# Expert layer of a two-layer decoder: where the first half's norms stand, two tiles opened in the attention before, a table of zeros filled later

## The chip, the cores and the metric

The kernel runs on one core of one Trainium2 chip. The metric is device time in microseconds of one launch. A core has five engines that work beside one another, each on its own queue in order: TensorE (PE, matrix products, with its weight loads shown apart as PEld), VectorE (DVE), ScalarE (ACT), GpSimd (POOL) and SyncE (SP, which here only issues transfers). An instruction waits at the head of its queue until the semaphores that it needs have been raised, and all behind it wait too. Data come and go by DMA engines.

## The reference, cut to what matters

The whole is a decoder of two layers on 16 sequences of 128 tokens, width 512: a state-space layer, a cross attention, a ternary feed-forward, a self attention, a gated attention over a memory, and a layer of experts. In the layer norm, `_layernorm`, mean and variance of a token are taken over the 512 values. The change touches the cross attention's start, the gated attention's end and the experts.

The experts come in 8 groups of 8. A router picks 8 experts for each token and gives each a weight. A token takes part in a group if one of its experts is in it: the token plus a mask projection (`mask_up_w`, chosen by which experts of the group were picked) goes through the group's gated product, `silu(g) * u` with inner width 352, and is brought back to 512. The results of its groups are weighed and added to the token, and the sum is normalised and written out.

## The kernel before

**Stages.** `stage_ssm`, `stage_xattn`, `stage_ffn`, `stage_attention` (self attention, then gated attention) and `stage_moe` follow one another. A sequence of 128 tokens is one tile of 128 partitions. The 16 sequences stay on the chip as `x`. Single precision products run in two passes, so that a product of 128x512 shows as two records.

**Who sets the order.** The kernel is written in generators. Each advances by one `yield` for each tick of the stage's loop, so that the jobs are mixed by hand. What is written is then ordered on each engine by a list scheduler, which may move an instruction a good deal ahead or back of its place in the text, with one exception: instructions passed to `tc.keep_in_program_order` stay among one another, and with what is around them, where they were written. Pools of buffers (`tile_pool`, `bufs=`) decide when a buffer comes free.

**Zeros.** `clear_rows` (L396) is a job that `stage_xattn` starts first (L642). It makes a table of zeros in memory, in eight transfers on SP's queue, and from the table fills the expert buckets: `bucket[half][group]`, 768 rows of 776 values, in six transfers each, and one row of each `results[half][group]`. In the same loop `project` (L479) loads the context `cT` of a sequence on SP's queue (L481), and makes `pk` and `pv` from it (L491). The keys are normalised and rotated on VectorE, ScalarE and GpSimd; the tables of cosine and sine come from `sincos` (L351 to L369).

**Experts.** The first half's tokens (sequences 0 to 7) are routed while the gated attention runs. `route` computes the weights, and GpSimd scatters each token's row to its group's bucket. Those of sequences 8 to 15 are routed in `stage_moe`. A row has 512 values, 256 picks, and 8 weights. The unit of work in `stage_moe` is a tile of 128 rows. There are 98 units: six for each of the 8 groups of both halves, but for the last group of the second half, which is done directly on the 8 sequences. Each unit goes through the steps below, and at tick t of the loop each step works on another unit, at a fixed lag:

```python
for lag, what in ((-5, m.fetch), (-1, m.turn_in), (0, m.gate_up), (1, m.turn_act), (-2, m.masks), (-3, m.places), (2, m.down), (2, m.store)):
```

`fetch` loads the row tile (`row`, six buffers, on SP). `places` turns the picks (`pts` on TensorE, `soft` on ScalarE). `masks` is the product `pm` on TensorE and the addition `xg` on VectorE. `turn_in` transposes (`ptx`, then `xgT` on ScalarE). `gate_up` makes `pg` and `pu` with sixteen passes, `Silu` on ScalarE and `act` on VectorE. `turn_act` transposes `act`. `down` makes `y`. `store` copies it to `yo` on VectorE and writes it to `results`.

When a group is done, `combine` (L1572) gathers the results per token on GpSimd (`got`) and, three parts later, adds them to `x` (L1584). For the last group and an odd sequence it goes on to `finish`: `layernorm` of two sequences on VectorE (20 instructions: two statistics each, the reciprocal root of `rsqrt`, two scalings) and two output transfers on SP. The scheduler is free to place these VectorE instructions. In the first half there are four such pairs.

The Moe object holds `k.to_route` (the sequences to be routed), `tick` and `send` (the parts of that job), and the weights of the first group (`m.first`), which are loaded in `stage_attention`. The pool of `stage_moe` is opened at its start, when those of the attention have been closed, and takes their memory; its row loads wait for that. Between the attention and the experts the row load of the first tile is issued on SP at 2459.91 us of the span.

Of the kernel before, what the change touches and what calls it, by code (L numbers as in the profile page):

```python
# [10 lines left out]
F32 = mybir.dt.float32  # L11
BF16 = mybir.dt.bfloat16
F32R = mybir.dt.float32r
I32 = mybir.dt.int32
U8 = mybir.dt.uint8
AF = mybir.ActivationFunctionType
ALU = mybir.AluOpType
# [3 lines left out]
P = 128  # L21
NB = 16
D = 512
# [19 lines left out]
        self.n += 1  # L43


def rsqrt(k, v, n, eps, scale=1.0):


    nc = k.nc
    a = k.small.tile([P, n], F32, tag=f"rs_a{n}", name="rs_a")  # L50
    y = k.small.tile([P, n], F32, tag=f"rs_y{n}", name="rs_y")
    t = k.small.tile([P, n], F32, tag=f"rs_t{n}", name="rs_t")
    nc.vector.tensor_scalar(a, v, scale, eps, ALU.mult, ALU.add)
    nc.vector.tensor_scalar(y.bitcast(I32), a.bitcast(I32), -0.5, 1597463007.0, ALU.mult, ALU.add)
    for _ in range(3):
        nc.vector.tensor_tensor(t, y, y, ALU.mult)
        nc.vector.scalar_tensor_tensor(t, t, -0.5, a, ALU.mult, ALU.mult)
        nc.vector.scalar_tensor_tensor(y, t, 1.5, y, ALU.add, ALU.mult)
    return y


def layernorm(k, ins, outs, eps=1e-5):

    nc, n = k.nc, len(ins)
    mv = k.small.tile([P, n, 2], F32, tag=f"ln_mv{n}", name="ln_mv")
    for i, r in enumerate(ins):
        st = k.small.tile([P, nc.vector.BN_STATS_DIM], F32, tag="ln_st", name="ln_st")
        nc.vector.bn_stats(st, r)
        nc.vector.bn_aggr(mv[:, i, :], st)
    rstd = rsqrt(k, mv[:, :, 1], n, eps)  # L70
    for i, (r, o) in enumerate(zip(ins, outs)):
        nc.vector.tensor_scalar(o, r, mv[:, i, 0:1], rstd[:, i : i + 1], ALU.subtract, ALU.mult)


def stage_ssm(k):
# [320 lines left out]
def clear_rows(k, pool):  # L396

    n = Moe.ROW // 8
    zero = pool.tile([P, n], F32, name="zero")
    k.nc.gpsimd.memset(zero, 0.0)  # L400
    for i in range(8):
        k.nc.sync.dma_start(k.zeros[:, i * n : (i + 1) * n], zero)
    yield
    for h in range(2):
        for bucket, result in zip(k.bucket[h], k.results[h]):
            k.nc.sync.dma_start(result[0:1], k.zeros[0:1, 0:D])
            for j in range(Moe.TILES):
                k.nc.sync.dma_start(bucket[j * P : (j + 1) * P], k.zeros)
                yield
# [830 lines left out]
def stage_attention(k):  # L1240

    nc, tc = k.nc, k.tc
    U = 8
    with ExitStack() as ctx:
        wk = ctx.enter_context(tc.tile_pool(name="s4w", bufs=2))
        own = ctx.enter_context(ExitStack())
        wr = own.enter_context(tc.tile_pool(name="s4r", bufs=2, side="right"))  # L1250
        pp = ctx.enter_context(tc.tile_pool(name="s4p", bufs=2, space=PSUM))
        psc = ctx.enter_context(tc.tile_pool(name="s4s", bufs=1, space=PSUM))
        ppt = ctx.enter_context(tc.tile_pool(name="s4t", bufs=1, space=PSUM))
        pao = ctx.enter_context(tc.tile_pool(name="s4o", bufs=1, space=PSUM))
        pools = wk, wr, pp, psc, ppt, pao
        pairs = [c(k, p, pools) for c in (SelfAttention, GatedAttention) for p in range(NB // 2)]
        units = [(pr, n) for pr in pairs for n in range(U)]

        begin = {}
        for m, pr in enumerate(pairs):  # L1260
            begin.setdefault(U * m - (14 if m < NB // 2 else 10), []).append(pr)
        running = [load_gated_weights(k)]
        first = [pairs[0].project(), pairs[1].project()]
        for n in range(12):
            next(first[0])
            if n >= 7:
                next(first[1])
        running.append(first[1])
        for t in range(-2, len(units) + 2):
            if k.moe:  # L1270
                k.moe.tick()
            for lag in (2, 1, 0, -1, -2):
                if not 0 <= t - lag < len(units):
                    continue
                pr, n = units[t - lag]
                if lag == pr.LAG:
                    pr.turn(n)
                    if n % 4 == 3:
                        running.append(pr.values(n // 4))
                if lag == 1:  # L1280
                    pr.norm(n)
                if lag == 0:
                    pr.exps(n)
                if lag == -1 and n % 2 == 0:
                    pr.top(n)
                if lag == -2 and n % 2 == 0:
                    pr.scores(n)
            if t == NB // 2 * U + 20:
                own.close()
                k.moe = Moe(k, pp)  # L1290
                running.append(k.moe.setup())
            for pr in begin.get(t, []):
                if t > -2:
                    running.append(pr.project())
            for job in list(running):
                if next(job, running) is running:
                    running.remove(job)
            if k.moe:
                k.moe.tick()
                k.moe.send()  # L1300
        while running:
            k.moe.tick()
            for job in list(running):
                if next(job, running) is running:
                    running.remove(job)
            k.moe.tick()
            k.moe.send()


class Moe:  # L1310
# [199 lines left out]


    def fetch(self, u):
        u.row = self.wk.tile([P, self.ROW], F32, tag="row", name="row", bufs=6)
        self.nc.sync.dma_start(u.row, u.src)

    def places(self, u):
        at = D + P * (u.g // 4)
# [3 lines left out]
        self.nc.scalar.copy(u.soft, pt)  # L1521

    def masks(self, u):
        pm = self.pm.tile([P, D], F32, tag="pm", name="pm")
        self.nc.tensor.matmul(pm, u.soft, self.mup[u.g], start=True, stop=True)
        u.xg = self.wk.tile([P, D], F32, tag="xg", name="xg")
        self.nc.vector.tensor_tensor(u.xg, pm, u.row[:, 0:D], ALU.add)
# [43 lines left out]
    def combine(self, h, g, n):  # L1571

        k, nc, b = self.k, self.nc, h * (NB // 2) + n
        got = self.wk.tile([P, D], F32, tag="got", name="got", bufs=10)

        end = 1 + min(P * (n + 1), self.CAP)
        nc.gpsimd.indirect_dma_start(  # L1577
            out=got[:, :], out_offset=None, in_=k.results[h][g][0:end, :],
            in_offset=bass.IndirectOffsetOnAxis(ap=self.gidx[:, b, g : g + 1], axis=0),
        )  # L1580
        yield
        yield
        yield
        nc.gpsimd.tensor_tensor(k.x[b], got, k.x[b], ALU.add)  # L1584
        for _ in range(4):
            yield
        if g == self.NG - 1 and n % 2:
            self.finish(b - 1)

    def finish(self, b):  # L1590
        xs = self.k.x[b : b + 2]
        layernorm(self.k, xs, xs)
        for i, x in enumerate(xs):
            self.nc.sync.dma_start(self.k.args["out"][b + i], x)


def stage_moe(k):


    nc, tc, m = k.nc, k.tc, k.moe  # L1600
    NG, T, H = m.NG, m.TILES, NB // 2
    with ExitStack() as ctx:
        m.wk = wk = ctx.enter_context(tc.tile_pool(name="s6w", bufs=2))
        wp = ctx.enter_context(tc.tile_pool(name="s6m", bufs=2))
        mp = ctx.enter_context(tc.tile_pool(name="s6u", bufs=1))
        m.pgu = ctx.enter_context(tc.tile_pool(name="s6g", bufs=1, space=PSUM))
# [3 lines left out]
        units, weights = [], {0: m.first}  # L1610
        for h in range(2):
            for g in range(NG):
                last = h and g == NG - 1
                for j in range(H if last else T):
                    u = Ctx()
                    u.h, u.g, u.j, u.b = h, g, j, H + j
                    u.src, u.to = (k.rows[u.b][:, :], None) if last else (
                        k.bucket[h][g][j * P : (j + 1) * P, :], k.results[h][g][1 + j * P : 1 + (j + 1) * P, :]
                    )
                    units.append(u)  # L1620
        running = []
# [3 lines left out]
                if next(job, running) is running:  # L1625
                    running.remove(job)

        for t in range(-5, len(units) + 4):
            if t == 3:
                k.to_route += range(H // 2, H)  # L1630
            m.tick()
            n = t + 8
# [4 lines left out]
            for lag, what in ((-5, m.fetch), (-1, m.turn_in), (0, m.gate_up), (1, m.turn_act), (-2, m.masks), (-3, m.places), (2, m.down), (2, m.store)):  # L1637
                if not 0 <= t - lag < len(units):
                    continue
                u = units[t - lag]  # L1640
                if what == m.fetch:
                    u.w = None
                if what == m.gate_up:
                    u.w = weights[u.h * NG + u.g]
                what(u)
            if 0 <= t - 3 < len(units) and units[t - 3].to is not None:
                u = units[t - 3]
# [17 lines left out]
        with tc.If(over > 0):  # L1665
            for b in range(NB):
                nc.sync.dma_start(k.x[b], k.rows[b][:, 0:D])
            for g in range(NG):
                w = m.load(wp, g)
                for b in range(NB):  # L1670
                    u = Ctx()
# [131 lines left out]
```

## Time and profile before

| what | value |
|---|---|
| three runs | 3347.26, 3347.7, 3352.11 us, median 3347.7 |
| profiled execution | 3354.11 us |
| its span | 3352.3 us (1.8 us lie around it) |
| mean granted TensorE clock | 0.969 |
| busy: PE, DVE, ACT, POOL | 94%, 56%, 41%, 41% of the span |
| cross attention begins | about 607 us |
| experts begin | about 2463 us |

A row of a timeline has start, duration, engine, line, operation, output and inputs, shape, and in square brackets the idle time ahead of it and the instruction or transfer that released it. A row of the waits has the sum, the number and the longest. A row of the windows has for each engine its busy time in a stretch; the clock is 1.00 at full speed, and the two last columns are DMA share and GB/s. The times of PE's ends are modelled, so neighbouring products overlap a little.

### The profile page before, as it was taken

How to read it: one execution, taken by the hardware profiler on the slowest of the kernel's cores; microseconds unless marked ns; L12 is line 12 of the kernel's file. 1: busy time of each engine (PE TensorE's matmuls, PEld its weight loads, DVE VectorE, ACT ScalarE, POOL GpSimd, SP SyncE). 2: the span in 40 equal slices, each digit the busy share in tenths (PEclk: the TensorE clock that was granted, in tenths of full speed). 3: DMA queues.
4: the chain of work that ended last, by engine and by line, in shares of the span. 5: the costliest groups of instructions: out<-in, count | busy, mean ns of one | idle time of the engine just before them, and what ended most of it. 6: DMA issues, size and time to landing. Idle time of an engine off the chain costs nothing.

```text
span 3352.3 us, 38574 instructions
## 1 busy us (share of the span) xinstructions
PE 3160.3 (94%) x12944; PEld 1814.2 (54%) x12944; DVE 1874.6 (56%) x4202; ACT 1381.0 (41%) x3299; POOL 1390.2 (41%) x1196
## 2 busy tenths in 40 slices
PE   6899998899999999999999899998989999999998
PEld 3444444355555555555566466665555566556665
DVE  5887788556456456455576589665643332322224
ACT  4655555233333333334433399765632322112221
POOL 6977886233333233232000265225624454233331
PEclk8999999899999999999999999998999999999999
DMA  6533332780000000002200100023345575445441
GB/s 231 135 80 96 85 87 63 242 293 4 7 4 7 4 4 7 4 1 101 85 1 1 63 1 1 14 71 135 136 144 181 190 242 198 156 157 171 162 157 64
DMA packets 162577, 317.28 MB, mean 95 GB/s; under 512 B 20233, under 2 KB 83209, under 8 KB 159300
## 3 DMA queue, kind: packets, MB, share of 16 engines
q1 hardware_dynamic: 124164, 216.23, 20.9%
q0 software_dynamic: 19200, 64.16, 5.6%
q10 hardware_dynamic: 19008, 34.35, 2.7%
q8 instruction: 105, 1.72, 0.2%
q14 instruction: 100, 0.82, 0.1%
HBM read 238.80 MB, written 129.04 MB: 110 GB/s over the span
## 4 chain that ended last, share of the span: by engine, by line
PE 64%; DVE 9%; ACT 3%; DMA 2%; issue 2%; POOL 2%; SPq 0%; ACTq 0%; POOLq 0%; DVEq 0%
PE pq L491 6%; PE y L1558 6%; PE pg L1541 6%; PE pu L1541 6%; PE po L614 6%; PE po L781 4%; PE pk L491 3%; PE ao L603 3%; PE sc L563 3%; PE pt L377 3%; PE pv L491 2%; PE ps L1142 2%; PE pg L767 2%; PE pu L767 2%; PE pT L591 1%
## 5 line engine op out<-in xcount | busy, mean ns | idle before, releaser
L245 POOL TENSOR_TENSOR dBx<-dtx,BC 128x1024 f32<-128x1024 f32 x128 | 301.9, 2378 | 33.2 <-DVE h L258 26.0
L1541 PE MATMUL pg<-gu,xgT 128*128 128x352 f32 x784 | 301.2, 466 | 0.0
L1541 PE MATMUL pu<-gu,xgT 128*128 128x352 f32 x784 | 300.4, 465 | 0.0
L1558 PE MATMUL y<-dn,aT 128*128 128x512 f32 x588 | 268.3, 592 | 0.0
L1545 DVE SCALAR_TENSOR_TENSOR act<-pu,row,act 128x352 f32<-128x352 f32 x98 | 57.1, 583 | 377.2 <-PE pu L1541 319.0
L583 POOL TENSOR_TENSOR pr<-pr,sm 128x512 f32<-128x512 f32 x128 | 134.7, 1053 | 289.5 <-DVE sm L582 235.0
L236 ACT ACTIVATE h<-dt,negA 128x254 f32<-128x254 f32 x512 | 239.9, 474 | 15.0 <-DVE dt L178 2.1
L1584 POOL TENSOR_TENSOR x<-got,x 128x512 f32<-128x512 f32 x120 | 152.3, 1275 | 224.5 <-DMA got<-results,gidx 220.4
L614 PE MATMUL po<-w,aT 128*128 128x512 f32 x512 | 230.6, 593 | 0.5 <-DVE aT L608 0.5
L491 PE MATMUL pq<-w,xT 128*128 128x512 f32 x512 | 228.9, 594 | 0.0
L1577 POOL DMA_INDIRECT got<-results,gidx x120 | 116.2, 968 | 270.1 <-DMA results<-yo 193.9
L468 POOL TENSOR_TENSOR m<-m,m 128x512 f32<-128x512 f32 x96 | 121.6, 1267 | 244.0 <-DVE m L463 244.0
L576 ACT ACTIVATE pr<-sc,mx,sf 128x256 f32<-128x256 f32 x256 | 142.9, 562 | 188.1 <-DVE mx L569 175.8
L258 DVE TENSOR_TENSOR_SCAN h<-h,dBx 128x1024 f32<-128x1024 f32 x80 | 183.3, 2294 | 57.7 <-ACT h L236 43.1
L267 PE MATMUL py<-hC,ident 128*128 128x512 f32 x320 | 167.9, 654 | 41.6 <-ACT y L272 35.5
L1541 PEld LDWEIGHTS pu<-gu,xgT 128*128 128x128 f32 x784 | 151.1, 193 | 84.9 <-issue 3.8
L1541 PEld LDWEIGHTS pg<-gu,xgT 128*128 128x128 f32 x784 | 144.1, 194 | 65.1 <-issue 3.7
L1544 ACT ACTIVATE act<-pg 128x352 f32<-128x352 f32 x98 | 45.5, 464 | 317.9 <-PE pg L1541 249.6
L1558 PEld LDWEIGHTS y<-dn,aT 128*128 128x128 f32 x588 | 104.1, 190 | 100.8 <-issue 94.0
L1533 ACT COPY xgT<-ptx 128x512 f32<-128x512 f32 x98 | 57.5, 587 | 232.9 <-PE ptx L377 206.1
L491 PEld LDWEIGHTS pq<-w,xT 128*128 128x128 f32 x512 | 93.5, 190 | 102.0 <-issue 99.0
L614 PEld LDWEIGHTS po<-w,aT 128*128 128x128 f32 x512 | 94.7, 190 | 95.3 <-issue 91.8
(363 smaller groups left out, 6824.0 us busy)
## 6 DMA issues: line engine op xcount, KB each, us to landing
bucket<-zeros SPq DMA_DIRECT2D x96, 388.0 KB
row<-bucket SPq DMA_DIRECT2D x90, 388.0 KB
BC<-bcd SPq DMA_DIRECT2D x128, 256.0 KB
results<-yo ACTq DMA_DIRECT2D x90, 256.0 KB
gu<-in_moe_guT SPq DMA_DIRECT2D x16, 1408.0 KB
cT<-in_ctxT SPq DMA_DIRECT2D x32, 256.0 KB
dn<-in_moe_downT SPq DMA_DIRECT2D x16, 512.0 KB
rows<-r_row SPq DMA_DIRECT2D x16, 388.0 KB
```

Source lines behind the costliest of these rows:

```text
L236: nc.scalar.activation(h[:, c, :, 1:], st.dt[:, c].rearrange("p (b t) -> p b t", b=BQ)[:, :, 1:], AF.Exp, scale=negA[:, c, n : n + 1])
L245: nc.gpsimd.tensor_tensor(dBx, st.dtx, BC[:, 0].unsqueeze(1).to_broadcast([P, KC, TQ]), ALU.mult)
L258: nc.vector.tensor_tensor_scan(hf, hf, df, 0.0, ALU.mult, ALU.add)
L267: nc.tensor.matmul(st.py[c], k.ident, st.hC[n][:, 2 * c : 2 * c + 2], start=n == 0, stop=n == NS - 1)
L491: nc.tensor.matmul(ps, src[:, c], w[c], start=c == 0, stop=c == KC - 1)
L576: nc.scalar.activation(pr[:, j], st.sc[g, i][:, j], AF.Exp, scale=st.sf[:, h : h + 1], bias=st.mx[g, i][:, j : j + 1], accum_out=sm[:, j : ...
L583: nc.gpsimd.tensor_tensor(pr, pr, sm.unsqueeze(2).to_broadcast([P, 2, 2 * P]), ALU.mult)
L614: nc.tensor.matmul(st.po, aT[:, j], k.wo[h // 8][:, h % 8], start=h == 0, stop=h == G * J - 1)
L767: nc.tensor.matmul(p, sn.qT[i][:, c], w[:, c, h * D : (h + 1) * D], start=c == 0, stop=c == KC - 1)
L1541: nc.tensor.matmul(ps, u.xT[:, c], gu[:, c, lo : lo + I], start=c == 0, stop=c == KC - 1)
L1558: self.nc.tensor.matmul(u.y, u.aT[:, c], u.w[1][:, c], start=c == 0, stop=c == 2)
L1584: nc.gpsimd.tensor_tensor(k.x[b], got, k.x[b], ALU.add)
```

## The change

There are three parts. `finish` for the first half is written two parts later, and with the rest of the norm is held to its written place by `keep_in_program_order`. `Moe.open`, a new job, is started in `stage_attention` eight units before the end of its loop: it opens a pool of its own with room for two rows, fetches the first two tiles and does `places`, `masks` and `turn_in` for both, with the attention's accumulators; `stage_moe` leaves out these steps for them and starts its loop at −3 instead of −5. And `clear_rows` yields three times before it fills the table of zeros. The arithmetic is the same. On TensorE some 90 places at the border of attention and experts change their order; on VectorE the norms' instructions stand later; on SP the first `cT` load stands ahead of the eight transfers of zeros.

```diff
 def clear_rows(k, pool):
     n = Moe.ROW // 8
+    for _ in range(3):
+        yield
     zero = pool.tile([P, n], F32, name="zero")
...
+            if t == len(units) - 8:
+                assert not (k.moe.now or k.moe.sending or k.to_route)
+                running.append(k.moe.open())
         while running:
...
     def fetch(self, u):
-        u.row = self.wk.tile([P, self.ROW], F32, tag="row", name="row", bufs=6)
+        u.row = self.wk.tile([P, self.ROW], F32, tag="row", name="row", bufs=self.depth)
         self.nc.sync.dma_start(u.row, u.src)
+
+    def open(self):
+
+        self.wk = self.k.moe_ctx.enter_context(self.k.tc.tile_pool(name="s6o", bufs=2, side="right"))
+        self.pm, self.depth, self.opened = self.pp, 2, []
+        for j in range(2):
+            u = Ctx()
+            u.g, u.src = 0, self.k.bucket[0][0][j * P : (j + 1) * P, :]
+            self.opened.append(u)
+            self.fetch(u)
+        yield
+        yield
+        for link in (self.places, self.masks, self.turn_in):
+            for u in self.opened:
+                link(u)
+                yield
...
         if g == self.NG - 1 and n % 2:
-            self.finish(b - 1)
-
-    def finish(self, b):
+            for _ in range(2):
+                yield
+            self.finish(b - 1, k.tc.keep_in_program_order)
+
+    def finish(self, b, keep=lambda ins: ins):
         xs = self.k.x[b : b + 2]
-        layernorm(self.k, xs, xs)
+        layernorm(self.k, xs, xs, keep=keep)
...
-        m.wk = wk = ctx.enter_context(tc.tile_pool(name="s6w", bufs=2))
+        m.wk, m.depth = ctx.enter_context(tc.tile_pool(name="s6w", bufs=2)), 6
...
-                    u = Ctx()
+                    u = Ctx() if len(units) >= len(m.opened) else m.opened[len(units)]
...
-        for t in range(-5, len(units) + 4):
+        for t in range(-3, len(units) + 4):
...
                 u = units[t - lag]
+                if u in m.opened and what in (m.fetch, m.places, m.masks, m.turn_in):
+                    continue
```

In `layernorm` and `rsqrt` each VectorE instruction is passed through `keep`; their default leaves it as it is.

More of the change, by code (lines that the diff above doesn't have):

```diff
@@ L43, in __call__, with rsqrt @@
         self.n += 1
-def rsqrt(k, v, n, eps, scale=1.0):
+def rsqrt(k, v, n, eps, scale=1.0, keep=lambda ins: ins):
     nc = k.nc
@@ L52, in rsqrt, with layernorm @@
     t = k.small.tile([P, n], F32, tag=f"rs_t{n}", name="rs_t")
-    nc.vector.tensor_scalar(a, v, scale, eps, ALU.mult, ALU.add)
-    nc.vector.tensor_scalar(y.bitcast(I32), a.bitcast(I32), -0.5, 1597463007.0, ALU.mult, ALU.add)
+    keep(nc.vector.tensor_scalar(a, v, scale, eps, ALU.mult, ALU.add))
+    keep(nc.vector.tensor_scalar(y.bitcast(I32), a.bitcast(I32), -0.5, 1597463007.0, ALU.mult, ALU.add))
     for _ in range(3):
-        nc.vector.tensor_tensor(t, y, y, ALU.mult)
-        nc.vector.scalar_tensor_tensor(t, t, -0.5, a, ALU.mult, ALU.mult)
-        nc.vector.scalar_tensor_tensor(y, t, 1.5, y, ALU.add, ALU.mult)
+        keep(nc.vector.tensor_tensor(t, y, y, ALU.mult))
+        keep(nc.vector.scalar_tensor_tensor(t, t, -0.5, a, ALU.mult, ALU.mult))
+        keep(nc.vector.scalar_tensor_tensor(y, t, 1.5, y, ALU.add, ALU.mult))
     return y
-def layernorm(k, ins, outs, eps=1e-5):
+def layernorm(k, ins, outs, eps=1e-5, keep=lambda ins: ins):
     nc, n = k.nc, len(ins)
@@ L67, in layernorm @@
         st = k.small.tile([P, nc.vector.BN_STATS_DIM], F32, tag="ln_st", name="ln_st")
-        nc.vector.bn_stats(st, r)
-        nc.vector.bn_aggr(mv[:, i, :], st)
-    rstd = rsqrt(k, mv[:, :, 1], n, eps)
+        keep(nc.vector.bn_stats(st, r))
+        keep(nc.vector.bn_aggr(mv[:, i, :], st))
+    rstd = rsqrt(k, mv[:, :, 1], n, eps, keep=keep)
     for i, (r, o) in enumerate(zip(ins, outs)):
-        nc.vector.tensor_scalar(o, r, mv[:, i, 0:1], rstd[:, i : i + 1], ALU.subtract, ALU.mult)
+        keep(nc.vector.tensor_scalar(o, r, mv[:, i, 0:1], rstd[:, i : i + 1], ALU.subtract, ALU.mult))
 def stage_ssm(k):
@@ L1523, in masks @@
     def masks(self, u):
-        pm = self.pm.tile([P, D], F32, tag="pm", name="pm")
+        pm = self.pm.tile([P, D], F32, tag="pp" if self.pm is self.pp else "pm", name="pm")
         self.nc.tensor.matmul(pm, u.soft, self.mup[u.g], start=True, stop=True)
```

## The prediction, made before the changed kernel had run

> **What bounds the kernel now.** I read the page first (span, slices, chain), then TensorE's waits, then the timeline round the three longest waits that the change touches, and last the granted clock there. Line numbers are those of the kernel before.
>
> ```profile
> span 3352.3 us, 38574 instructions
> PE   6899998899999999999999899998989999999998
> PEclk8999999899999999999999999998999999999999
> PE 64%; DVE 9%; ACT 3%; DMA 2%; issue 2%; POOL 2%; SPq 0%; ACTq 0%; POOLq 0%; DVEq 0%
> ```
>
> TensorE is busy in nearly every slice and carries most of the chain. So an edit pays only where TensorE stands still, or runs at a lower clock after having stood still. Its waits, in all and at the longest:
>
> ```profile
> PE ptx L377 <- DVE xg L1527: 18.7, 9, 6.8
> PE pk L491 <- DMA results<-zeros: 13.2, 1, 13.2
> PE pts L1519 <- DMA row<-bucket: 5.1, 1, 5.1
> PE ptx L377 <- ACT r_x L1410: 4.4, 1, 4.4
> ```
>
> The first three are the norms, the zeros and the start of the experts: one for each part of the change. The norms, on the timeline (start, duration, idle before and its releaser):
>
> ```profile
> 2904.88 1.27 POOL L1584 TENSOR_TENSOR x<-got,x 128x512 f32<-128x512 f32 x1 [6.00 <-DMA got<-results,gidx]
> 2906.18 0.69 DVE L68 BATCH_NORM_STATS2 ln_st<-x 128x6 f32<-128x512 f32 x1 [7.78 <-POOL x L1584]
> 2909.91 0.63 PE L377 MATMUL ptx<-ident,xg 128*128 128x128 f32 x4 [2.75 <-DVE xg L1527]
> ...
> 2936.20 3.73 POOL L1584 TENSOR_TENSOR x<-got,x 128x512 f32<-128x512 f32 x3 [1.27 <-DMA got<-results,gidx]
> 2937.50 0.69 DVE L68 BATCH_NORM_STATS2 ln_st<-x 128x6 f32<-128x512 f32 x1 [6.26 <-POOL x L1584]
> 2946.81 1.09 PE L377 MATMUL ptx<-ident,xg 128*128 128x128 f32 x4 [6.81 <-DVE xg L1527]
> ```
>
> Read it as a chain: VectorE has a norm at the head of its queue and waits for GpSimd's last addition. Behind the norm stand act and xg of the running tiles, and TensorE waits for xg. Five ptx waits lie here (0.72, 2.75, 0.72, 1.83, 6.81 us). The clock pays again:
>
> ```profile
> 2911.00:2914.40 3.40, 3.40 (x7) 1.92 (x6) 0.00 (x0) 0.22 (x1) 0.59 (x1) 0.51 0.33 122
> 2945.20:2952.00 6.80, 5.19 (x12) 3.48 (x13) 2.06 (x4) 0.59 (x1) 1.26 (x1) 0.50 0.73 249
> ```
>
> The column before the last two is the clock: half speed for 3.4 us after the gap of 2.75, for 6.8 us after that of 6.81.
>
> **Part C, the norms (17.5 us).** From the ptx at 2889.25 to the one at 2957.82 are 68.57 us for six tiles; an undisturbed tile takes 8.42 us (2957.82 to 2966.24). 68.57 − 6 × 8.42 = 18.05 us lost: 12.83 in the five waits, the rest by the clock. After the change the norms keep their written place, and in the changed program's order each pair's norm stands about ten tiles later, near 2990 and on. The last addition ended at 2939.93, so nothing is waited for. The same instructions run, 20 on VectorE a pair; in an earlier block they take 0.69 + 0.18 for one tile and then 4.12 us from the second BATCH_NORM_STATS2 to the end, about 4.9 us. They go into this hole of VectorE:
>
> ```profile
> 2958.02 0.69 DVE L1568 COPY yo<-y 128x512 f32<-128x512 f32 x1 [1.99 <-PE y L1558]
> 2963.25 0.58 DVE L1545 SCALAR_TENSOR_TENSOR act<-pu,row,act 128x352 f32<-128x352 f32 x1 [4.54 <-PE pu L1541]
> ```
>
> A hole of 4.54 us takes a block of 4.9 with some 0.4 left over. Act and xg are that much later; xg ends at 2964.44, and TensorE needs it for the load at 2965.81, 1.4 us of slack. Two of the four blocks may cost 0.4 us if they are interleaved worse. The eight output transfers move on SP to a place ahead of a later row load, which is due five tiles ahead: nothing. Gain 18 − 0.5 = 17.5, range 14 to 18.
>
> **Part B, two tiles opened early (8 us).**
>
> ```profile
> 2458.62 1.26 POOL L1230 TENSOR_TENSOR x<-x,gate 128x512 f32<-128x512 f32 x1 [5.65 <-DVE gate L1229]
> 2459.91 1.27 SPq L1514 DMA_DIRECT2D row<-bucket  x3
> 2462.96 0.45 PE L1519 MATMUL pts<-ident,row 128*128 128x128 f32 x1 [5.15 <-DMA row<-bucket]
> ```
>
> The row loads wait for the attention's buffers, and so for its last GpSimd operation; TensorE is idle from 2457.81. Then it goes 0.40 and 0.48 us idle between pts, pm and ptx, with the clock at half from about 2460.5 to 2470.7. In the changed order the rows of tiles 0 and 1 are fetched while the gated attention runs. That attention's loads have come by then, and the scatter that fills the bucket is issued for the last time at 2412.62, some 23 us before TensorE reaches the new pts (behind the transposes at 2435.34). Ahead of the attention's end TensorE gets 2 pts (0.22), 2 pm (0.62), 2 ptx of four transposes each (0.86) and half of tile 0's gate and up (2.37), 4.07 us. Of that about 3.7 falls into its small waits there (0.87, 1.42, 0.73, 0.70 us), so the attention ends about 0.35 later. The other half of gate and up (2.37) runs in the idle 5.15. Tile 1 then waits for VectorE's act of tile 0, which is ordered inside the attention's last norm, until about 2463.7, and for the row of tile 2, which is still issued behind the last GpSimd operation.
> What before has reached at 2476.15 is reached some 11 us earlier if only work counts. Two takings off: a shorter clock loss remains (a gap of about 2 us), and the row of tile 3 queues behind gu and dn (1408 and 704 KB on SP), which land near 2470: 3 us. Net 8, from 4 (only the 5.15 us less a new wait) to 11.
>
> **Part A, the zeros (0.5 us).**
>
> ```profile
> 610.04 8.15 SPq L402 DMA_DIRECT2D zeros<-zero  x8
> 618.24 0.43 SPq L481 DMA_DIRECT2D cT<-in_ctxT  x1
> 621.33 6.75 PE L491 MATMUL pk<-w,cT 128*128 128x512 f32 x8 [13.17 <-DMA results<-zeros]
> ...
> 639.43 0.66 PE L377 MATMUL pt<-ident,m 128*128 128x128 f32 x4 [0.34 <-POOL m L526]
> ```
>
> Eight issues on SP, 8.15 us, and the small packets behind them stand ahead of cT, the real releaser of pk. Put ahead of them, cT comes only behind the second weight load, which fills the queues until about 614.3: pk starts at about 617.2, 4.1 earlier. But the next wait is already there: the second pt (639.43) needs GpSimd's m, at the end of a chain through cos and sin on VectorE and ScalarE. That chain does not start earlier, and by the new order a square (ScalarE) and a reduction (0.68 us on VectorE) go ahead in it. I give pt 2.0 us, and TensorE a new gap of 2 to 3.7 before it.
> Here the clock must be weighed. The rows above have half clock after a gap of 2.75, and the gap at 2417.8 to 2420.9 (3.2) had half clock for 10.2 us. The Trainium skill, "TensorE: Matmul & The Clock Gate", section "HAM oscillation", has the rule "no PE-idle gaps >~3.4µs". By the rule part A's gap is free and A brings 2.0; by the rows it costs 3.4 us at half clock, 1.7 us, and A brings about 0.5. By the rule part B's second gap would also be free, and the sum 29. I take the rows: 0.5, from −2 to +2.5.
> The zeros table itself is filled later, and its readers, the bucket fills, are 96 transfers with no reader before the attention: hidden.
>
> **The sum.** 17.5 + 8 + 0.5 = 26 us, against the profiled execution's 3354.11 (span 3352.3): 3328.1. The median of the runs is 3347.7, 6.4 us below that execution, so 3321.7, say 3322. Ends of the parts together: 14 + 4 − 2 = 16 (3332) and 18 + 11 + 2.5 = 31.5 (3316).
>
> **Rivals.**
> 1. The opened tiles bring nothing (chance 0.15): tile 2's row, or act of tile 0 behind the norm, is the last wait at the same time as before. For it: the row is issued at 2459.91 in any case. Against it: 4 to 5 us of TensorE work fills that wait. Gain 17.5 + 0 + 0.5, 3330.
> 2. The norms only move their stall (0.10): blocks of 4.9 us in a hole of 4.54, now held together in order, cost 2 us a block and with it a clock drop of 1.7 for two of them: C brings 18 − 8 − 3.4 = 6.6, the sum 15, 3333. Against it: 1.4 us of slack behind the hole.
> 3. Slower (0.05): the second half's routing runs beside the first thirty tiles, and its ScalarE copies wait for the bucket scatters on GpSimd's queue. Two such stalls are there now (4.42 at 2565.96, 4.81 at 2645.87, with 3.4 and 6.8 us of half clock). The change shifts these copies and the preparation of the expert masks by a few places. A stall with its clock costs up to 4.81 + 3.4 = 8.2 us; from four more on, 33 us, the gain of 26 is gone and the kernel ends near 3355. Against it: their order relative to the scatters is unchanged.
> 4. The three waits close just about and the losses meet (0.05): no change, within 6.7 us of 3347.7. 0.2% is about what a measurement here can tell from nothing; the three runs spread over 0.15%.
> The forecast itself has 0.65.
>
> **How the numbers follow.** Faster by over 0.2%: forecast, rivals 1 and 2, 0.90. Within: 0.05. Slower: 0.05. The range 3312 to 3335 takes in the parts' ends and rivals 1 and 2, with 4 us below for clock gains that I have not counted (the clock of 0.969 over the span), and leaves out rivals 3 and 4.
>
> **What would show it.** Right: no ptx wait on xg over 1 us between the four norm blocks, which stand without a GpSimd releaser; tile period 8.42 us all along there; TensorE busy between 2458 and 2462 on pg and pu; pk of the first sequence near 617 with pt on m still a wait. Wrong: a new wait of ptx on xg about ten tiles later (rival 2), an idle TensorE ahead of the pts of tile 2 of 5 us as before (rival 1), more waits on r_x or xg between 2500 and 2700 (rival 3).

## The result, and the profile after

The changed kernel takes 3324.78 us (median of 6 runs, 3320.85 to 3331.42), before 3347.48 (6 runs, 3346.27 to 3353.86): 22.7 us less, a ratio of 0.9928 (95% interval 0.9916 to 0.9940). The forecast was 3322, the range 3312 to 3335. The two profiled executions differ by more: spans of 3352.3 and 3322.3 us. The reason is told with the stage table below. Line numbers past L398 are now 2 to 25 higher.

The waits of TensorE after (in all, times, longest):

```profile
PE ptx L377 <- DVE xg L1548: 9.6, 3, 4.8
PE pk L493 <- DMA zeros<-zero: 9.4, 1, 9.4
PE pv L493 <- DVE m L465: 3.6, 1, 3.6
PE pts L1540 <- DMA row<-bucket: 2.5, 3, 1.3
```

All three waits of before have shrunk (18.7, 13.2 and 5.1 us), and one is new: pv waits 3.6 us for m. The 9.6 us that ptx still waits are none of the norms': 0.50 us lie at the start of the experts, 4.32 and 4.78 in tiles 10 to 30, where the kernel before waits 4.42 and 4.81.

**The norms.** The stretch of tiles 46 to 53, which held the five waits, first in the kernel before and then in the changed one, and behind it the stretch of the changed kernel where the norms now stand (length, then busy time of PE, PEld, DVE, ACT, POOL, then the clock):

```profile
2886.27:2963.25 76.98, 64.15 (x220) 37.85 (x218) 28.19 (x88) 11.34 (x28) 21.24 (x19) 0.93 0.44 149
...
2874.25:2933.21 58.96, 58.96 (x221) 35.88 (x218) 13.23 (x22) 11.88 (x28) 19.96 (x18) 1.00 0.47 156
...
2940.00:3010.00 70.00, 70.00 (x261) 42.74 (x260) 34.05 (x94) 14.69 (x35) 23.54 (x21) 1.00 0.57 190
```

Before, TensorE stood idle for 12.83 of the 76.98 us and had a mean clock of 0.93; now it is busy all the time at full clock in both windows. The norms show in VectorE's 34.05 us of the last window: in the one of the same length from 2840 to 2910 it is busy for 16.32. The first block, on VectorE's timeline:

```profile
2953.24 0.69 DVE L1589 COPY yo<-y 128x512 f32<-128x512 f32 x1 [2.00 <-PE y L1579]
2953.85 0.68 DVE L68 BATCH_NORM_STATS2 ln_st<-x 128x6 f32<-128x512 f32 x1
...
2957.75 1.00 DVE L72 TENSOR_SCALAR x<-x,ln_mv,rs_y 128x512 f32<-128x512 f32 x2
2958.66 0.58 DVE L1566 SCALAR_TENSOR_TENSOR act<-pu,row,act 128x352 f32<-128x352 f32 x1
2959.16 0.68 DVE L1548 TENSOR_TENSOR xg<-pm,row 128x512 f32<-128x512 f32 x1
```

No bracket stands behind the statistics: nothing was waited for. Act follows at once, 0.2 us later than the rhythm of 8.42 us (it came at 2950.05 for the tile before). That is what overflowed from the hole.

**The opened tiles.** TensorE at the border:

```profile
2456.64 0.86 PE L1562 MATMUL pg<-gu,xgT 128*128 128x352 f32 x2 [1.36 <-ACT act L1565]
...
2458.38 0.30 PE L1540 MATMUL pts<-ident,row 128*128 128x128 f32 x1 [0.88 <-DMA row<-bucket]
...
2466.30 0.33 PE L1540 MATMUL pts<-ident,row 128*128 128x128 f32 x1 [1.32 <-DMA row<-bucket]
```

The idle of 5.15 us has become 1.36 and 0.88: first TensorE waits for ScalarE's Silu, ahead of which a table load of 1.28 us stands at 2454.83, then for the row of the third tile. A later row waits 1.32 us more.

**The zeros.** TensorE at the start of the cross attention:

```profile
615.61 5.25 PE L493 MATMUL pk<-w,cT 128*128 128x512 f32 x8 [9.38 <-DMA zeros<-zero]
...
627.86 5.37 PE L493 MATMUL pv<-w,cT 128*128 128x512 f32 x8 [3.56 <-DVE m L465]
```

pk starts 3.8 us earlier after the stage's first transposes (10.0 us behind them, not 13.8). It stands still again before pv.

**By stages.** The same stretches in the traces of nine executions, each from one event to the next: from the first transposes of the cross attention (pt of x) to its first pq; on to the self attention's last x; to the last gate of the gated attention; to act of tile 10; to tile 30, 46, 53; to the last act. All in us.

| kernel | to pq | to last x | to last gate | to tile 10 | 10 to 30 | 30 to 46 | 46 to 53 | 53 to end |
|---|---|---|---|---|---|---|---|---|
| before | 32.4 | 1538.0 | 279.9 | 106.8 | 186.9 | 134.7 | 77.0 | 369.6 |
| changed | 31.8 | 1536.4 | 279.2 | 99.5 | 187.1 | 134.7 | 59.0 | 369.7 |
| changed again | 31.8 | 1536.6 | 275.8 | 98.8 | 185.4 | 134.7 | 59.0 | 369.7 |
| norms alone | 31.5 | 1540.7 | 279.3 | 106.6 | 187.5 | 134.7 | 59.0 | 369.7 |
| two tiles opened alone | 31.3 | 1535.9 | 278.1 | 101.7 | 193.0 | 134.7 | 76.3 | 369.7 |
| zeros alone | 31.7 | 1536.6 | 275.0 | 105.7 | 193.1 | 134.7 | 76.4 | 369.7 |
| norms unpinned | 32.5 | 1537.8 | 283.0 | 107.0 | 185.2 | 134.7 | 76.3 | 369.7 |
| norms without yields | 31.6 | 1537.5 | 278.8 | 107.0 | 187.1 | 134.7 | 59.0 | 369.7 |
| one tile opened | 31.8 | 1536.6 | 279.9 | 101.6 | 187.5 | 134.7 | 59.0 | 369.7 |

Ahead of the first column the state-space stage ends at 605.6 to 609.8 us, whatever the kernel. That time and the second, third and fifth columns vary by 4 to 8 us between executions in which their code is the same. That is the kernel's spread; the profiled pair had 1.9 us of it in the state-space stage and 2.4 in the second and third columns, which is part of why the spans differ by 30 and the medians by 22.7. Where the change works, the columns are far steadier: 46 to 53 is 76.3 to 77.0 or 58.95 to 58.96, and the step to tile 10 takes 105.7 to 107.0 us with none opened; with two opened it takes 98.4 to 102.2 over all eight traces.

### The profile page after: what moved, and what is told of

Read it like the earlier page. It is cut to its first block, busy times and chain, and to the rows that moved or that the text cites. A ratio compares the mean times of both kernels' runs of the same rounds, so it can differ in the third digit from the quotient of the medians.

```text
span 3322.3 us, 38519 instructions
## 1 busy us (share of the span) xinstructions
PE 3145.9 (95%) x12894; PEld 1811.7 (55%) x12944; DVE 1872.8 (56%) x4202; ACT 1379.3 (42%) x3299; POOL 1388.4 (42%) x1196
## 5 line engine op out<-in xcount | busy, mean ns | idle before, releaser
L1589 DVE COPY yo<-y 128x512 f32<-128x512 f32 x90 | 62.1, 690 | 156.7 <-PE y L1579 145.7
```

## The experiments

**Each part alone.** Norms alone:

```diff
-            self.finish(b - 1)
+            for _ in range(2):
+                yield
+            self.finish(b - 1, k.tc.keep_in_program_order)
```

> The kernel before with the norms' part alone (two yields later, VectorE instructions held in their written place). Theory: the norms were placed ahead of GpSimd's last additions and held act and xg behind them; in their written place they wait for nothing. 18 us less than before (3347.5 to about 3329.5), no ptx wait on xg over 0.5 us past 2880 us of the span, tile period 8.42 us throughout. Rival (the stall only moves to the new place of the norms): 7 to 12 us less, with waits of 1 to 2 us at ptx some ten tiles later and a clock drop beside two of them.

Measured: 3335.77 us beside 3353.01 for before on the same chip, ratio 0.9951 (0.9938 to 0.9963), 12 to 21 us less. The stretch from 46 to 53 falls from 77.0 to 59.0, no ptx waits past tile 46. The norms' gain is 17.3 to 18.0 us, and the rival's second stall isn't there.

Two opened tiles alone (`open` called, the loop starting at −3; norms and zeros as before):

> The kernel before with the two opened tiles alone. Theory: TensorE fills the wait for the first rows with prepared work: 7 us less than before (about 3340.5); of the attention's end to tile 10 of the experts 7 us less in the traces. Rival (the row of the third tile and act of the first are the last waits in any case): 0 to 2 us less, and an idle of about 5 us ahead of the third tile's pts.

Measured: 0.9990 (0.9980 to 1.0000), 0 to 7 us less. To tile 10 it takes 101.7, against 105.7 to 107.0: 4 to 5 us. In the changed kernel it was 99.5. The row of a later tile came late here (3.62 us of wait at 2470.56 against 1.32). Of the eight traces with two tiles opened one other has this late row (3.68 us; the run with the tables early and the output weights in front), and these two take 101.7 and 102.2 us to tile 10, the other six 98.4 to 99.8. The theory's sign holds; its size does where the row isn't late, and why it is late in two executions was not tried.

Zeros alone:

```diff
     n = Moe.ROW // 8
+    for _ in range(3):
+        yield
     zero = pool.tile([P, n], F32, name="zero")
```

> The kernel before with the later filling of the zeros table alone. Theory: pk starts 4 us earlier, but the chain of cosine and sine sets the next products, so that from the stage's first transposes to its first pq only 0.6 us are saved: time within 2 us of before. Rival (the zeros' transfers were what the stage waited for): 4 us less, and 4 us less from the first transposes to the first pq.

Measured: 0.9992 (0.9983 to 1.0002), between 6 us less and 1 more. To the first pq it takes 31.7 us, with the zeros as before 31.3 to 32.5: nothing that can be told. pk is at 9.9 instead of 13.8 us, and the wait of 3.55 us at pv takes it back. The rival falls.

**What bounds the cross attention's start?** The load of the output weights was held behind the small loads, on top of the changed kernel:

```diff
-    load_xattn_weights(k, 1)
...
         for t in range(-12, len(units) + 4):
+            if t == -8:
+                load_xattn_weights(k, 1)
...
-            nc.sync.dma_start(k.wo[i], ...)
+            k.tc.keep_in_program_order(nc.sync.dma_start(k.wo[i], ...))
```

> The changed kernel with the two loads of the cross attention's output weights (2 MB each) held behind the small loads of positions, frequencies and norm weights and behind the first two cT loads. Theory: what is left at the start of the cross attention is the chain of cosine and sine, which waits for small loads behind 4 MB of weights: it starts some 5 us earlier, and so do pk and the first pq; 4 to 6 us less than the changed kernel, about 3319. Rival (the chain is not the bound, cT or the accumulators are): within 2 us of the changed kernel. A second one: the small loads wait for the state-space stage's buffers in any case (they are issued at about 607 us): 0 to 3 us less.

Measured: 0.9932 (0.9919 to 0.9944), the same as the changed kernel. TensorE:

```profile
609.82 5.37 PE L492 MATMUL pk<-w,cT 128*128 128x512 f32 x8 [1.64 <-DMA cT<-in_ctxT]
...
627.88 5.21 PE L492 MATMUL pv<-w,cT 128*128 128x512 f32 x8 [9.26 <-DVE m L464]
```

pk now starts 2.3 us behind the stage's first transposes, in the changed kernel 10.0, and TensorE waits at pv 9.26 instead of 3.56. To the first pq it takes 29.7 us, a gain of 2. So cT isn't the bound. My own theory of 4 to 6 us fell too. The tables' chain began 5.6 us behind the transposes instead of 9.3, so 3.7 of the 5 us sooner: its small loads are still issued only 1.1 and 1.6 us behind the transposes, when the state-space stage has released memory, as the second rival says. And from there to the first m it takes 13.2 us instead of 11.5, since VectorE has the key's reductions and reciprocal root between the rows of the chain.

So the loads of positions and frequencies were moved into that stage, with 512 bytes of their own:

```diff
     if part == 0:
+        k.sincos = SinTables(k, k.trig_pool, None)
...
-        sincos = SinTables(k, cst, wk)
+        sincos = k.sincos
+        sincos.wk = wk
...
+    k.trig_pool = ctx.enter_context(tc.tile_pool(name="trig", bufs=1))
     for stage in STAGES:
```

> As the run with the later output weights, and the loads of positions and frequencies for the cosine and sine tables are taken in the state-space stage into 512 bytes of their own, so that VectorE's chain for the tables can start before the last output of that stage. The run before it moved pk to 609.8 us of the span, but TensorE then waited 9.26 us at pv for m, the end of that chain. Theory (the chain is the bound of the cross attention's start): that wait goes to under 3 us, the first pq comes 20 to 24 us after the stage's first transposes (31.8 in the changed kernel), and the time is 7 to 11 us under the changed kernel's, about 3316. Rival (the chain waits for memory of the state-space stage or for its last products, and cannot start before 607): within 3 us of the changed kernel.

Measured: 3317.07 us, 0.9897 (0.9880 to 0.9913), against 0.9926 and 0.9928 for the changed kernel: 8 to 10 us less than it, and the fastest version here. To the first pq it takes 23.9 us. The chain starts at 608.78, 0.8 us ahead of the first transposes. What remains:

```profile
611.73 3.67 PE L494 MATMUL pk<-w,cT 128*128 128x512 f32 x8 [1.50 <-DMA cT<-in_ctxT]
...
623.97 5.37 PE L494 MATMUL pv<-w,cT 128*128 128x512 f32 x8 [5.14 <-DVE m L466]
```

The wait at pv is 5.14, not under 3: the state-space stage's last norm is interleaved with the chain on VectorE (the reciprocal root between the rows of `ang`). The chain is still the bound.

The same with the output weights left in front:

> The changed kernel with the early loads of positions and frequencies alone; the output weights stay ahead of cT. Theory: now cT behind 4 MB of weights is the bound: pk starts at about 615.6 as in the changed kernel, the wait of 3.56 us at pv is gone, and the first pq comes 28 us after the stage's first transposes. Rival (the chain does not start earlier): 31 to 32 us.

```profile
619.56 5.91 PE L495 MATMUL pk<-w,cT 128*128 128x512 f32 x8 [9.32 <-DMA zeros<-zero]
```

In one execution it took 27.7 us to the first pq, with no wait at pv. With the tables early, cT behind the weights is the bound: the row names the zeros as the releaser, but the run above differs in the weights' place alone, and there pk starts 7.8 us sooner behind the transposes, released by cT.

And this with the zeros put ahead of cT again:

> As the run with the early tables and the output weights first, without the later filling of the zeros: the eight transfers of zeros are ahead of cT again. In that run the first pq came 27.7 us after the stage's first transposes. Theory (the later filling is worth 4 us once the chain of cosine and sine is not the bound): about 31.5 us here, pk released by the transfers of zeros near 13 us after the transposes. Rival (it is worth nothing in any case): 27 to 28 us.

In one execution it took 30.2 us. The later filling, not to be told from nothing in the changed kernel, is worth 2.5 us here (4 expected). pk starts 2.9 us later, and between pk and pq 17.4 us pass instead of 17.7. It is one execution against one; the five with the zeros first and the tables late spread over 1.2 us (31.3 to 32.5).

**Which half of the norms' edit does it?** With the two yields alone, norms left to the scheduler:

> The kernel before with the norms written two parts later, but left to the scheduler. Theory (the held place does it, not the two yields): the norms stand as far ahead as before, the five ptx waits on xg of 12.8 us stay, time as before. Rival (the two yields do it): 15 to 18 us less.

Measured: 1.0008 (0.9998 to 1.0018). The old wait stands at its old place:

```profile
2947.65 1.09 PE L377 MATMUL ptx<-ident,xg 128*128 128x128 f32 x4 [6.62 <-DVE xg L1527]
```

And with the held place alone, without the yields:

> The kernel before with the norms held in their written place, but without the two yields more. Theory: the place is some two tiles (17 us) ahead of that of the changed kernel and still behind the last addition at about 2940 us: 17 to 18 us less than before, as with the yields. Rival (two parts earlier the block meets act and xg, or the additions): a gain of 8 to 14 us with ptx waits of 1 us and more.

Measured: 0.9939 (0.9922 to 0.9956), 46 to 53 in 58.95 us. The first norm stands 3.8 us behind act of tile 53, in the changed kernel, with the yields, 20.6. Holding the place is the whole gain; the two parts later bring nothing.

**One tile opened instead of two** (`range(1)` in `open`, the loop from −4):

> The changed kernel with one tile opened in the gated attention instead of two (the experts' loop starts one tick earlier for it). Theory (work prepared ahead fills the wait for the first rows): from the attention's last gate product to act of tile 10 it takes 100 us with two tiles opened and 106.5 with none; with one it lies between, about 103, and TensorE is idle 2 to 3 us more ahead of the second tile's pts; time 2 to 4 us over the changed kernel. Rival (the rows' arrival alone sets the tenth tile): 100, no more time.

```profile
2461.27 0.45 PE L1540 MATMUL pts<-ident,row 128*128 128x128 f32 x1 [4.22 <-DMA row<-bucket]
```

To tile 10 it takes 101.6, between the means of 106.6 with none opened and 99.1 in the changed kernel's two traces. The idle ahead of the next row is 4.22 us, 3.3 more than with two (0.88). The time is 0.9939 (0.9921 to 0.9958), which the interval doesn't part from the changed kernel's. Against the six traces with two tiles opened whose later row wasn't late (98.4 to 99.8) the second tile brings 2 to 3 us, and most of the gain comes with the first. But the two with the late row (101.7 and 102.2) are no better than this one, so that one execution of it doesn't settle the size.

**Gaps of chosen length, for the clock** (further statistics on VectorE ahead of xg in six tiles):

```diff
+        for _ in range(late):
+            st = self.k.small.tile([P, self.nc.vector.BN_STATS_DIM], F32, tag="ln_st", name="ln_late")
+            keep(self.nc.vector.bn_stats(st, u.row[:, 0:D]))
-        self.nc.vector.tensor_tensor(u.xg, pm, u.row[:, 0:D], ALU.add)
+        keep(self.nc.vector.tensor_tensor(u.xg, pm, u.row[:, 0:D], ALU.add))
```

> The changed kernel with VectorE held up ahead of xg in six tiles of the steady stretch (tiles 32 to 42 of the first half, every other one), by 4, 5, 6, 7, 8 and 9 statistics instructions of about 0.66 us whose results are not used. With 1.75 us of slack the waits at ptx should be about 0.9, 1.6, 2.2, 2.9, 3.5 and 4.2 us. By the rule of no idle gap over 3.4 us only the last two are followed by half clock; by the rows of the kernel before (2.75 us followed by 3.4 us of half clock) the last three are, and perhaps the third. Each gap is to be read in the granted clock of the 10 us behind it.

It missed: no gap came. VectorE was held up as wished, but in the order that the scheduler made, ptx stands behind six of the eight pairs of pg and pu passes of the tile ahead, not in front of them:

```profile
2825.32 5.43 DVE L1555 BATCH_NORM_STATS2 ln_late<-row 128x6 f32<-128x512 f32 x9
2831.40 0.66 PE L377 MATMUL ptx<-ident,xg 128*128 128x128 f32 x4
```

Tiles 30 to 46 took 135.3 us instead of 134.7. Yet this execution shows something of the clock by chance. In the same code at the start of the cross attention, TensorE waited 3.04 us at pv here, and 3.56 in the second run of the changed kernel. Behind the first the clock stayed full, behind the second it was at half for 3.4 us. To the first pq it took 29.6 us here, and 31.7 to 31.8 in the four others with the later zeros alone at this place.

It isn't the length of the gap that decides. In all fourteen traces half clock starts and ends on a grid of steps of 3.41 us, which keeps its place for the whole execution and has another place in each. Cut at these steps, the wait at pv reads as follows, here and in the second run of the changed kernel (the first figure behind the comma is TensorE's busy time in the step, the clock is third from the right):

```profile
626.47:629.88 3.41, 1.92 (x5) 0.57 (x3) 2.16 (x4) 2.17 (x4) 2.25 (x5) 1.00 0.92 350
629.88:633.29 3.41, 1.86 (x5) 0.94 (x6) 3.33 (x8) 0.00 (x0) 3.20 (x7) 1.00 1.01 306
633.29:636.71 3.42, 3.42 (x10) 1.51 (x9) 3.08 (x11) 0.58 (x1) 1.80 (x3) 1.00 0.92 298
```

```profile
626.93:630.34 3.41, 1.21 (x3) 0.68 (x4) 2.71 (x7) 0.62 (x2) 2.99 (x6) 1.00 0.95 284
630.34:633.76 3.42, 3.42 (x5) 1.35 (x4) 3.15 (x9) 0.00 (x0) 2.45 (x4) 0.50 0.93 290
```

Here the wait leaves two steps busy for 1.92 and 1.86 us, over half of each. There pv starts 0.65 us later behind the transposes, a step is left with 1.21 us, 35% busy, and the next is at half clock. The gap of 2.75 us in the kernel before (first row) left 1.14 us of its step, and half clock followed from 2911.05. At the experts' border of the changed kernel (second and third row) two waits of 1.36 and 0.88 us left 1.17, and half clock followed too:

```profile
2907.64:2911.05 3.41, 1.14 (x7) 0.96 (x8) 1.23 (x3) 1.42 (x4) 0.97 (x1) 1.00 0.46 154
...
2455.17:2458.58 3.41, 1.17 (x4) 0.43 (x3) 2.81 (x13) 1.41 (x2) 0.00 (x0) 1.00 0.73 251
2458.58:2462.00 3.42, 3.34 (x7) 2.15 (x7) 1.89 (x5) 0.27 (x1) 0.00 (x0) 0.50 1.03 393
```

Counted over the fourteen traces past 600 us: of the steps at full clock in which TensorE was busy for less than 40%, all 143 were followed by a step at half clock; of those with 70% or more, one of 10,331. In between it was 74 of 225, and what decides there stays open.

**The changed kernel again:**

> The changed kernel once more, beside the others on one chip: 0.9928 of before (0.9916 to 0.994) as measured, and in its trace 17.6 us less from tile 46 to tile 53, 100 us from the last gate product to tile 10, and 31.5 to 32 us from the first transposes of the cross attention to the first pq.

Measured: 0.9926 (0.9910 to 0.9943), and 59.0, 98.8 and 31.8 us in the three stretches.

## Why the prediction was right

**Norms, 17.5 forecast, 17.3 to 18.0 measured.** The mechanism held: VectorE waiting for GpSimd was the cause (the held place alone removes it, the yields alone don't), the norms stand about ten tiles later (2953.85, which is 2984 in the time of the kernel before), and the hole takes them. The overflow was put at 0.4 us for two of the blocks (0.8 us, of which the sum takes off 0.5). Act came 0.2, 0.6 and 0.8 us late in three tiles, and TensorE lost nothing, since 1.4 us of slack were there.

**Opened tiles, 8 forecast, about 7 measured** (106.6, the mean of five traces with none opened, less 99.5). The idle of 5.15 went to 1.36 and 0.88, and the half clock from 10 us to one of 3.4 (2458.58 to 2462.00). The 3 us set aside for late rows were 2.5 in all: 0.88, 1.32 and 0.32. One term can't be told: the attention was to end 0.35 us later for the inserted work, and its stretch is 279.2 us against 279.9, within a spread of 8. And tile 1 waited for ScalarE's Silu (1.36 us), where the forecast has it wait for VectorE's act. Rival 1 is excluded, as the row of the third tile was the last wait only after the work had filled most of it.

**Zeros, 0.5 forecast, nothing measured (31.8 against 31.3 to 32.5).** pk was to start 4.1 us earlier and came 3.8 earlier. A gap of 2 to 3.7 us was foreseen and was 3.56. But I had it ahead of pt, and it is ahead of pv: two accumulators serve pk and pv, and pv needs the one that m's products read. The chain behind it is the one named, and the two runs that start it sooner show that it was the bound.

**The clock.** By the rule that the prediction takes from the Trainium skill ("TensorE: Matmul & The Clock Gate", section "HAM oscillation"), no gaps over about 3.4 us, the zeros bring 2.0 us if their gap stays below; by the rows of before 0.5. Both readings price a gap by its length, and the traces show that length doesn't decide: gaps of 2.75 and 3.56 us were followed by half clock, so were 1.36 and 0.88 in one step, and 3.04 wasn't. In four of the five executions with the later zeros the wait at pv left a step 35 to 37% busy, half clock followed, and nothing was gained; in the fifth the wait left two steps over half busy, and 2.1 us were gained. So that part A came out near 0.5 and not 2.0 was in part luck: the figure was right, the reason given for it wasn't.

**The sum.** 26 forecast; 18 + 7 + 0 = 25 by the stages; 22.7 by the medians, where an interval of 20 to 28 us hangs on the spread above. Rival 2 is excluded by the windows at full clock. Rival 3's stalls exist: tiles 10 to 30 take 185.2 to 193.1 us. But 193 is also seen with the zeros alone, which touch nothing there, and 185.4 in the changed kernel, so the traces don't tie it to the change. In the three traces of 193 a third wait of 5.8 us at ptx stands right behind act of tile 11, beside the two long ones of the others. What brings it about in an execution was not tried.

## What to carry to other kernels

A scheduler that places work of low urgency early can put an instruction that still has to wait at the head of an engine's queue; look for the waits behind it, and hold it to a late place rather than write it later. Before a load is brought forward, ask which chain joins it at the next product: the 4 us won at pk were worth nothing in most executions until the chain of cosine and sine was brought forward too, and that together with the later weights' load gave 8 us. And when executions differ by more than an edit is worth, cut the traces at the same events and compare stretch by stretch.

## What I had not expected of the hardware

The same code waited 3.04 us in one execution and 3.56 in another, and the stage took 2.1 us more in the second. Half clock followed how much of a step of 3.41 us TensorE had stood idle, not how long one gap was: two waits of 1.36 and 0.88 us were enough where they fell into one step. And an unchanged state-space stage ended anywhere from 605.6 to 609.8 us, so that one profiled pair showed 30 us where the medians show 22.7.
